# A four-layer graph attention stack: list pieces moved out of the head, lists three row tiles ahead, masks kept as bits

## The chip, the cores and the metric

The kernel runs on one core of a Trainium2 chip. The metric is the device time of one execution in microseconds (us). Five engines work side by side, each through its own queue of instructions: PE (TensorE, matmuls), DVE (VectorE), ACT (ScalarE), POOL (GpSimd, which here issues the indirect gathers) and SP (SyncE, which here issues most of the other DMAs).

## The reference

N = 4096 nodes with F = 256 features, and an adjacency matrix `adj` that is a random 1/256 of all pairs plus the diagonal, so that a row has about 17 neighbours. Four attention layers follow each other, each inside `x = layernorm(x + layer(x))`. Every layer has this form (layer 0 is shown; layer 1 is alike, layer 2 has two heads of 128 and biases, layer 3 has one score, a positive and a negative softmax over `x` itself, a matrix product and an ELU):

```python
h = (x @ W.T).reshape(4096, 4, 64).transpose(1, 0, 2)
e = alpha_src[:, :, None] + alpha_dst[:, None, :]      # two inner products of h per head
e = jnp.where(e >= 0, e, 0.2 * e)
e = jnp.where(adj[None, :, :] == 0, -jnp.inf, e)
attn = jax.nn.softmax(e, axis=-1)
out = jnp.einsum('hij,hjd->hid', attn, h)              # 4 heads of 64, put side by side
```

The same `adj` masks all four layers.

## The kernel before

**Tiles.** The 4096 nodes are 32 row tiles of 128 rows; four row tiles make a block. Instead of all 4096 columns, a row tile works on lists of the columns that its 128 rows need. A class `Projection` makes the projected rows of one row tile (values, scores and, in layer 0, the adjacency bits of that node) and stores them in the memory tables `vals` and `edge`. A class `RowTile` loads the rows on the lists of one row tile: one direct load of its own 128 rows and 13 indirect gathers on POOL (L763) of 128 rows each, into the buffers `G`. It works in two halves: half 0 reads its own rows and 6 gathers from the first 23 row tiles' rows (MIX = 23), half 1 has 7 gathers from all rows. For each half DVE and ACT form the scores (L871, L876, L880), DVE applies the mask (L837), and PE multiplies by the gathered values (L898). `finish` normalises the row tile, and the projection of the next layer follows.

**The lists.** `lists()` is a generator that builds, block by block and row tile by row tile, the list of columns. For a block: `fetch` loads the raw int32 adjacency (DMAs of 512 KB on SP, 4 buffers), `bytes` turns it to bytes on ACT (L393), `squeeze` folds bytes to bits on DVE (L405) and, for blocks with whole rows, stores the bytes in `maskW`; `sort`, `count`, `add` and `starts` make the counts. For a row tile: `ranks`, `steps`, `spread` (PE), `compare` (DVE, L504), `sum` (26 small matmuls, L516 and L518), and `write` (DVE, L522), which writes the 13 columns of `idx` that the gathers of that row tile read. Each `next(lists)` does one piece. The first five pieces load the block of row tiles 0 to 3 and the first part of the next block; four pieces follow for each row tile.

**The head.** `Program.run` first makes the 32 projections of layer 0, six steps each (transpose, copy, multiply, row, edge, store), as a software pipeline of 37 turns. 21 pieces of the generator (5 + 4 LEAD, LEAD = 4) are woven into these turns. Then the loop over the row tiles of layer 0 takes two pieces for each half, so the lists stay LEAD row tiles ahead. In layer 0, `Layer.part` starts the loads of row tiles up to m + 2 when row tile m is worked on; in the other layers up to m + 1.

**Masks.** In layer 0 the adjacency bits come with the gathered rows. `unpack` spreads them to bytes in a PSUM bank (L798, three instructions per half); a copy of the bank goes to `mk` (L822), and `mk` is stored to `maskC` in memory (L824). Layers 1 to 3 load `mk` from `maskC` (L757); layer 1 copies it to the bank (L826), and layers 2 and 3 multiply by it where it lies.

**Whole rows.** A few blocks of layers 1 to 3 (`WHOLE`: block 7; blocks 3, 7 and 6; blocks 7 and 6) are computed over all 32 column tiles without lists, woven between the row tiles (L1170 to L1181, and L1241 to L1246 for layer 1). Their masks are loaded as bytes from `maskW`, 512 KB for every four column tiles (`mw`).

**Order.** Each engine runs its instructions in the order in which the build placed them. That order isn't the order of the source: the tile scheduler takes an instruction ahead of others where its operands and its output buffer let it. Waits between engines and for DMAs are semaphores that the scheduler adds.

Of the kernel before, what the change touches and what calls it, by code (L numbers as in the profile page):

```python
# [50 lines left out]
P = 128  # L51
# [31 lines left out]
LEAD = 4  # L83
MIX = 23
CAP = NPAIR * P
BW = BT * P // 32
# [35 lines left out]
@with_exitstack  # L122
def kernel(ctx: ExitStack, tc: tile.TileContext, ins: dict, out: bass.AP):
    nc = tc.nc
    const = ctx.enter_context(tc.tile_pool(name="const", bufs=1))
    dram = ctx.enter_context(tc.tile_pool(name="xs", bufs=1, space=DRAM))
    ident = const.tile([P, P], F32, name="ident")
    make_identity(nc, ident)
    shared = {
        "ident": ident,  # L130
        "idx": const.tile([P, NT, NP], I32, name="idx"),
        "mhalf": const.tile([P, BT], F32, name="mhalf"),
        "flag": const.tile([1, 1], I32, name="flag"),
        "shift1": const.tile([P, 1], F32, name="shift1"),
        "shift2": const.tile([P, 1], F32, name="shift2"),
        "shift30": const.tile([P, 1], F32, name="shift30"),
        "shift3": const.tile([4, 4], F32, name="shift3"),
        "zero": const.tile([4, 4], F32, name="zero"),
        "maskC": dram.tile([NT, P, NU, P], U8, name="maskC"),
        "maskW": dram.tile([NB, P, NT, BT, P], U8, name="maskW"),  # L140
        "d": [const.tile([P, NT, TERMS[n]], F32, name=f"d{n}") if WHOLE[n] else None for n in range(4)],
        "v": [[dram.tile([N + 1, ROW[n]], F32, name=f"vals{n}{c}") for c in range(1 if n else 2)] for n in range(4)],
        "e": [dram.tile([NT, TERMS[n], P], F32, name=f"edge{n}") for n in range(4)],
        "x": [None] + [dram.tile([N, F], F32, name=f"xp{n}") for n in (1, 2, 3)],
    }
    nc.vector.memset(shared["mhalf"], -0.5)
    nc.vector.memset(shared["shift1"], -KEXP)
    nc.vector.memset(shared["shift2"], -2.0 * KEXP)
    nc.vector.memset(shared["shift30"], -3.0 * KEXP)

    nc.vector.memset(shared["zero"], 0.0)
    nc.vector.memset(shared["shift3"], -2.0 * KEXP)
    nc.gpsimd.affine_select(out=shared["shift3"], in_=shared["shift3"], pattern=[[1, 4]], compare_op=ALU.is_gt,
                            fill=0.0, base=0, channel_multiplier=-1)
    with ExitStack() as packed:
        Program(tc, packed, ins, out, shared).run()
    general = nc.values_load(shared["flag"][0:1, 0:1], min_val=0, max_val=1,
                             skip_runtime_bounds_check_because="it is the result of a comparison")
    with tc.If(general > 0):
        dense_layers(tc, ins, out, ident)  # L160
# [18 lines left out]
class Program:  # L179
# [99 lines left out]
    def lists(self, ctx):  # L279
# [62 lines left out]
        pat = cst.tile([P, 8, P // 32], I32, name="pat")  # L342
# [16 lines left out]
        shared["pat"] = pat  # L359
# [13 lines left out]
        class Block:  # L373
# [21 lines left out]
            def squeeze(self, part):  # L395
                js = slice(part * JG, (part + 1) * JG)
                if any(self.blk in w for w in WHOLE):
                    nc.sync.dma_start(out=shared["maskW"][self.blk, :, js], in_=self.mk)
# [9 lines left out]
                if part == BT - 1:  # L408
                    rows = shared["v"][0][self.blk % 2][:N, :BW].rearrange("(j p) w -> p j w", p=P)
                    nc.sync.dma_start(out=rows, in_=self.bits.rearrange("p j t w -> p j (t w)").bitcast(F32))  # L410

# [188 lines left out]
    def run(self):  # L600
# [3 lines left out]
        for n in range(4):  # L604
            for v in self.shared["v"][n]:
                nc.sync.dma_start(out=v[N:N + 1, :], in_=nothing[:, :ROW[n]])
        w0 = self.weights(0)
        layer = Layer(self, 0)
        with ExitStack() as ctx:
            lists = self.lists(ctx)  # L610
            xs = []
            for q in range(NT // 2):
                if q % 4 == 0:
                    slot = self.g0.tile([P, SLOT], F32, name="G")
                c = 2 * F * (q % 4)
                nc.sync.dma_start(out=slot[:, c:c + 2 * F].rearrange("p (t f) -> p t f", t=2),
                                  in_=to_tiles(ins["x"][2 * q * P:2 * (q + 1) * P, :]))
                xs += [slot[:, c:c + F], slot[:, c + F:c + 2 * F]]

            line = [Projection(self, 0, w0, x, m, (self.ptwo[0], self.ptwo[1], self.pmask)) for m, x in enumerate(xs)]  # L620
            turns, ahead, listed = NT + 5, BT + 1 + 4 * LEAD, 0
            for m in range(turns):
                while listed < ahead and listed * turns <= m * ahead:
                    next(lists)
                    listed += 1
                for k, step in enumerate(Projection.STEPS):
                    if 0 <= m - k < NT:
                        step(line[m - k])

# [8 lines left out]
        self.mwp = self.pool("mwp", 2)  # L638
# [5 lines left out]
        layer.close(None)  # L644


class Projection:
# [61 lines left out]
    def store(self):  # L709
        n, nc, T = self.n, self.nc, TERMS[self.n]  # L710
        erow = self.prog.io.tile([4, P], F32, name="erow")
        shift = self.shared["shift3"] if n < 3 else self.shared["zero"]
        nc.scalar.activation(erow[:T, :], self.pe[:T, :P], AF.Identity, bias=shift[:T, LOGS[n]:LOGS[n] + 1])
        nc.sync.dma_start(out=self.shared["e"][n][self.m], in_=erow[:T, :])
# [8 lines left out]
class RowTile:  # L723
# [23 lines left out]
    def load(self, half):  # L747
# [4 lines left out]
        if half == 0:  # L752
            self.S = prog.ld.tile([P, H4, P], F32, name="S")
            nc.sync.dma_start(out=self.S[:, :TERMS[n]], in_=sh["e"][n][m].partition_broadcast(P))
            self.mk = prog.ld.tile([P, NU, P], U8, name="mk")
            if n > 0:
                nc.sync.dma_start(out=self.mk, in_=sh["maskC"][m])  # L757
# [22 lines left out]
    def unpack(self, half, words):  # L780

        nc, pat = self.layer.nc, self.layer.shared["pat"]
        rows = self.slot(half, 0)[:, :HALF * ROW[0]].bitcast(I32).rearrange("p (k c) -> p k c", k=HALF)
        bits = rows[:, :, self.m % BT * (P // 32):(self.m % BT + 1) * (P // 32)]
        own = 1 - half
        two = 2 * len(PAIRS[half])
        for s in range(2):
            u = PAIRS[half][0]
            self.spread(words[:, u:u + two // 2, s * P // 8:(s + 1) * P // 8],
                        bits[:, own + s:own + two:2], pat[:, 4 * s:4 * (s + 1)])  # L790
        u, k = FULL[half][0], 0 if own else two
        count = len(FULL[half])
        self.spread(words[:, u:u + count, :], bits[:, k:k + count], pat)

    def spread(self, words, bits, pat):
        count, planes = bits.shape[1], pat.shape[1]
        shape = [P, count, planes, P // 32]
        self.layer.nc.vector.tensor_tensor(  # L798
            words.rearrange("p t (k w) -> p t k w", k=planes),
            bits.rearrange("p t (o w) -> p t o w", o=1).to_broadcast(shape),  # L800
            pat.rearrange("p (o k) w -> p o k w", o=1).to_broadcast(shape), op=ALU.bitwise_and)

    def half(self, half):
# [8 lines left out]
        first = half * UNITS[0]  # L812
        mh = self.mk[:, first:first + U, :]
        if n < 2:
# [4 lines left out]
            kept = mh.rearrange("p t i -> p (t i)").bitcast(I32)  # L819
            if n == 0:  # L820
                self.unpack(half, there.rearrange("p (t i) -> p t i", t=U))
                nc.vector.tensor_scalar(kept, there, 0, None, op0=ALU.bitwise_or)  # L822
                if half == 1:
                    nc.sync.dma_start(out=sh["maskC"][self.m], in_=self.mk)  # L824
            else:
                nc.vector.tensor_scalar(there, kept, 0, None, op0=ALU.bitwise_or)  # L826
            mh = there.bitcast(U8)
            mh2 = mh.rearrange("p (o i) -> p o i", o=1).to_broadcast([P, 2, U * P])
        pairs = [prog.wp.tile([P, 2, UNITS[1], P], F32, name="w") for _ in range(H // 2)]
# [93 lines left out]
class Layer:  # L923
# [47 lines left out]
    def part(self, m, part):  # L971


        if part == 0:
# [3 lines left out]
            for q in range(m, m + (3 if self.n == 0 else 2)):  # L978
# [7 lines left out]
    def half_alone(self, m, part):  # L986
# [4 lines left out]
        second = m > NT - (LEAD if self.n == 0 else 6) and len(self.ready) > 1  # L991
# [144 lines left out]
    def whole_rows(self):  # L1136
# [3 lines left out]
        for blk in WHOLE[n]:  # L1140
            tiles = range(blk * BT, (blk + 1) * BT)
            S = prog.bk.tile([P, T, BT, P], F32, name="Sw")
            for it, m in enumerate(tiles):
                nc.sync.dma_start(out=S[:, :, it, :], in_=sh["e"][n][m].partition_broadcast(P))
            zs = [None] * BT
            for heads in groups:
                accs = [prog.bank(prog.pfour) for _ in range(BT)]
                c0, c1 = heads[0] * Wd, (heads[-1] + 1) * Wd
                vs, mws = {}, {}

                def fetch(j):
                    if j >= NT:
                        return
                    if j % JG == 0:
                        mws[j] = prog.mwp.tile([P, JG, BT, P], U8, name="mw")
                        nc.sync.dma_start(out=mws[j], in_=sh["maskW"][blk, :, j:j + JG])
# [5 lines left out]
                for j in range(NT):  # L1162
                    fetch(j + 4)
                    mj = mws[j - j % JG][:, j % JG, :, :]
# [32 lines left out]
    def whole_heads(self):  # L1197
# [7 lines left out]
        for blk in WHOLE[n]:  # L1205
# [9 lines left out]
            for h in range(A, T):  # L1215
                nc.vector.reciprocal(S[:, h], S[:, h])
                nc.vector.tensor_scalar(S[:, h], S[:, h], LEAST, HUGE, op0=ALU.mult, op1=ALU.min)
            z = prog.bk.tile([P, BT, H, Wd], F32, name="zh")
            for up, flat in TWOS:
                bu, bf = prog.bank(prog.pwhole), prog.bank(prog.pwhole)  # L1220
                vs, mws = {}, {}

                def fetch(j):
                    if j >= NT:
                        return
                    if j % JG == 0:
                        mws[j] = prog.mwp.tile([P, JG, BT, P], U8, name="mw")
                        nc.sync.dma_start(out=mws[j], in_=sh["maskW"][blk, :, j:j + JG])
# [5 lines left out]
                for j in range(NT):  # L1234
                    fetch(j + 4)
                    mj = mws[j - j % JG][:, j % JG, :, :]
# [20 lines left out]
            for it, m in enumerate(tiles):  # L1257
                self.finish(m, z[:, it].rearrange("p h c -> p (h c)"), self.load_x(m), None)

# [547 lines left out]
```

## Time and profile before

| | us |
|---|---|
| median of 3 runs (2065.28 to 2066.7) | 2065.5 |
| the profiled execution | 2071.33 |
| its span, from first to last record | 2069.6 |
| mean granted TensorE clock of it | 0.912 |
| half 1 of row tile 0: first gather | 165.34 |
| row tile 1, row tile 31 of layer 0: first gathers | 174.08, 680.78 |
| layer 1: first gather | 698.2 |

How to read it: the page gives the busy time of each engine and its share of the span. "idle before" of an instruction is the time in which its engine did nothing ahead of it, and what follows "<-" is what ended that time: an instruction of another engine, a DMA, or "issue" where the profile shows nothing that was waited for. L numbers are lines of the kernel before. A busy share over the whole span mixes stages: the head (up to 165 us), layer 0 (to about 698), layer 1 (to about 1160), layer 2 (to about 1540) and layer 3.

### The profile page before, as it was taken

The numbers are of one execution on the slowest core, as the hardware profiler recorded it, in microseconds if no ns is written. First come the engines' busy times: TensorE is split into PE (matmuls) and PEld (weight loads), VectorE is DVE, ScalarE is ACT, GpSimd is POOL, SyncE is SP. The second block draws the span as 40 slices with busy tenths as digits, with TensorE's granted clock in tenths as the row PEclk, the third lists the DMA queues.
The fourth block names the chain that finished last, engine by engine and source line by source line (L and its number), as shares of the span: only waits on it lengthen the run. The fifth ranks groups of instructions, "written<-read, shape, count | busy, mean of one in ns | idle before, by whom it ended". The sixth has DMA issues, their size and how long they took to land. (4 is left out here: it accounts for less than half of the span.)

```text
span 2069.6 us, 46290 instructions
## 1 busy us (share of the span) xinstructions
PE 1822.6 (88%) x15281; PEld 1509.8 (73%) x15281; DVE 1467.9 (71%) x4366; ACT 1500.9 (73%) x4659; POOL 1383.9 (67%) x1387
## 2 busy tenths in 40 slices
PE   4765798999899959989989998899998999999995
PEld 2444677777778859978878788788986677667773
DVE  2434888888888959977777867778876366575655
ACT  4436888888877948866767769878874687667873
POOL 0016777777777777777777767777762776666772
PEclk7666998989989979998999999999999899999998
DMA  8677999999986867766666766777875898888983
GB/s 287 177 187 253 316 300 328 269 294 318 328 207 179 236 197 201 207 191 188 192 187 187 203 176 187 231 209 229 233 205 188 262 297 274 261 289 276 294 254 109
DMA packets 297816, 486.59 MB, mean 235 GB/s; under 512 B 77815, under 2 KB 206940, under 8 KB 297565
## 3 DMA queue, kind: packets, MB, share of 16 engines
q1 hardware_dynamic: 218076, 251.50, 40.1%
q0 software_dynamic: 74880, 227.83, 38.0%
q10 hardware_dynamic: 4608, 4.20, 0.6%
q8 instruction: 123, 2.02, 0.4%
q14 instruction: 129, 1.05, 0.2%
HBM read 427.36 MB, written 55.99 MB: 234 GB/s over the span
## 5 line engine op out<-in xcount | busy, mean ns | idle before, releaser
L763 POOL DMA_INDIRECT G<-vals,idx x1352 | 1378.4, 1020 | 653.4 <-issue 348.9
L898 PE MATMUL bank<-G,w 128*64 128x130 f32 (+5 forms) x9156 | 943.5, 311 | 73.6 <-DVE w L837 64.2
L898 PEld LDWEIGHTS bank<-G,w 128*64 128x64 f32 (+1 forms) x9156 | 769.8, 162 | 226.3 <-DVE w L837 73.3
L880 ACT ACTIVATE w<-S,G 128x64 f32<-128x64 f32 (+1 forms) x3080 | 823.5, 351 | 133.2 <-DMA G<-vals,idx 84.2
L1181 PE MATMUL bank<-vw,pw 128*128 128x129 f32 (+1 forms) x2560 | 419.8, 322 | 17.5 <-DVE pw L1171 5.8
L1181 PEld LDWEIGHTS bank<-vw,pw 128*128 128x128 f32 x2560 | 374.1, 194 | 58.2 <-issue 16.0
L837 DVE SCALAR_TENSOR_TENSOR w<-w,bank 128x1024 f32<-128x1024 f32 (+1 forms) x240 | 322.5, 1344 | 13.0 <-ACT w L880 12.4
L673 PE MATMUL bank<-wext,xT 128*128 128x268 f32 (+3 forms) x640 | 188.3, 429 | 33.5 <-DVE row L699 24.1
L673 PEld LDWEIGHTS bank<-wext,xT 128*128 128x128 f32 x640 | 123.2, 210 | 61.2 <-DVE row L699 24.7
L847 ACT ACTIVATE w<-S,G 128x64 f32<-128x64 f32 (+1 forms) x329 | 105.3, 352 | 85.5 <-DMA G<-vals,idx 51.0
L1171 DVE SCALAR_TENSOR_TENSOR pw<-pw,mw 128x512 f32<-128x512 f32 x192 | 129.9, 687 | 36.9 <-ACT pw L1170 35.5
L1178 DVE TENSOR_TENSOR pw<-pw,mw 128x512 f32<-128x512 f32 x128 | 87.6, 688 | 96.1 <-ACT pw L1175 62.8
L393 ACT ACTIVATE mk<-raw 128x1024 uint8<-128x1024 int32 x128 | 130.3, 1051 | 32.6 <-DMA raw<-in_adjB_dram 32.3
L876 DVE TENSOR_TENSOR w<-S,G 128x384 f32<-128x384 f32 x180 | 92.4, 517 | 79.8 <-DMA G<-vals,idx 61.0
L1170 ACT ACTIVATE pw<-Sw,d 128x512 f32<-128x512 f32 x192 | 134.5, 710 | 15.5 <-PE bank L1181 10.2
L1244 PE MATMUL bank<-vw,pw 128*128 128x65 f32 x512 | 89.1, 257 | 19.9 <-issue 19.9
L1173 ACT ACTIVATE pw<-Sw,d 128x512 f32<-128x512 f32 x128 | 89.9, 708 | 19.3 <-DMA Sw<-edge 10.3
L1246 PE MATMUL bank<-pw,vw 128*65 128x128 f32 x512 | 99.5, 277 | 0.0
L1244 PEld LDWEIGHTS bank<-vw,pw 128*128 128x128 f32 x512 | 78.6, 194 | 27.6 <-issue 27.3
L1241 DVE SCALAR_TENSOR_TENSOR pw<-Sw,cw,mw 128x512 f32<-128x512 f32 x128 | 93.8, 740 | 0.0
L664 ACT COPY xT<-bank 128x256 f32<-128x256 f32 x128 | 46.3, 362 | 62.3 <-PE bank L659 41.0
L706 PE MATMUL bank<-ident,row 128*4 128x128 f32 (+2 forms) x128 | 37.6, 294 | 56.6 <-DVE row L693 30.5
(193 smaller groups left out, 1805.1 us busy)
## 6 DMA issues: line engine op xcount, KB each, us to landing
raw<-in_adjB_dram SPq DMA_DIRECT2D x128, 512.0 KB
G<-vals,idx POOLq DMA_INDIRECT x1352
mw<-maskW SPq DMA_DIRECT2D x36, 512.0 KB
vw<-vals SPq DMA_DIRECT2D x128, 128.5 KB
S<-edge SPq DMA_DIRECT2D x60, 256.0 KB
vals<-row SPq DMA_DIRECT2D x96, 134.0 KB
vw<-vals SPq DMA_DIRECT2D x96, 129.0 KB
xp<-y SPq DMA_DIRECT2D x96, 128.0 KB
```

Of the source, the lines that this page charges most:

```text
L393: nc.scalar.activation(self.mk[:, 2 * q:2 * q + 2], src, AF.Copy)
L673: nc.tensor.matmul(pp[:, :c1 - c0], self.xT[:, k, :], wext[:, k, c0:c1], start=(k == 0), stop=(k == KT - 1 and brow is None))
L763: nc.gpsimd.indirect_dma_start(out=self.row(half, k), out_offset=None, in_=self.values[:N + 1 if half else MIX * P, :], in_offset=bass.Ind ...
L837: nc.vector.scalar_tensor_tensor(pair, pair, LEAST, mh2, op0=ALU.max, op1=ALU.mult)
L847: nc.scalar.activation(w[0][:, u, rows], S[:, 0, rows], AF.Relu, bias=d(g, 0))
L880: nc.scalar.activation(w[h][:, u, rows], S[:, h, rows], AF.Exp, bias=d(g, h))
L898: nc.tensor.matmul(a, w[h][:, u, rows], b, start=half == 0 and u == 0 and (n == 3 or h == turns[0][0]), stop=half == 1, skip_group_check=True)
L1170: nc.scalar.activation(p, S[:, h], AF.Exp, bias=d)
L1171: nc.vector.scalar_tensor_tensor(p, p, LEAST, mj, op0=ALU.max, op1=ALU.mult)
L1181: nc.tensor.matmul(accs[it][:, c:c + Wd], p[:, it, :], v[:, c:c + Wd], start=(j == 0 and h == heads[0]), stop=(j == NT - 1), skip_group_ch ...
L1244: nc.tensor.matmul(bu[:, it * Wd:(it + 1) * Wd], p[up][:, it, :], v[:, up * Wd:(up + 1) * Wd], start=j == 0 and it == 0, **how)
L1246: nc.tensor.matmul(bf[:Wd, it * P:(it + 1) * P], v[:, flat * Wd:(flat + 1) * Wd], p[flat][:, it, :], start=j == 0 and it == 0, **how)
```

## The change

- `LEAD` goes from 4 to 3, and layer 0 starts loads up to row tile m + 1 instead of m + 2. A constant `LATE` keeps the 4 that another condition took from `LEAD`.
- Nine list pieces (block of row tiles 0 to 3, the first part of the next, and row tile 0's own list) are woven into the first 24 turns of the head; the other eight of the 17 pieces follow when all projections have been issued.
- The x tiles of the head come in 6 loads instead of 16; the zero rows of `vals` are stored from ACT's queue instead of SP's; layer 0's `edge` rows are stored four row tiles at a time (8 stores instead of 32).
- `maskC` and `maskW` (bytes) become `bitsC` and `bitsW` (32-bit words of bits). A row tile's bits take 28 words a partition instead of bytes for all columns; a block's bits take 256 KB and are loaded once for each whole unit.
- In layer 0, `unpack` first copies the bits out of the gathered rows into a tile `bits` and stores it; the spread to bytes reads `bits`, and nothing is copied back from PSUM. In layers 1 to 3 the spread is done again for every half (three instructions), and once for every column tile of a whole unit (`bytes`).

The number of gathers (1352) is the same. The core of the diff:

```diff
-LEAD = 4
+LEAD = 3
+LATE = 4
...
-        "maskC": dram.tile([NT, P, NU, P], U8, name="maskC"),
-        "maskW": dram.tile([NB, P, NT, BT, P], U8, name="maskW"),
+        "bitsC": dram.tile([NT, P, 2 * HALF, MW], I32, name="bitsC"),
+        "bitsW": dram.tile([NB, P, NT, BT, MW], I32, name="bitsW"),
...
-            turns, ahead, listed = NT + 5, BT + 1 + 4 * LEAD, 0
+            turns, soon, listed = NT + 5, BT + 5, 0
             for m in range(turns):
-                while listed < ahead and listed * turns <= m * ahead:
+                while listed < soon and listed * 24 <= m * soon:
                     next(lists)
                     listed += 1
                 for k, step in enumerate(Projection.STEPS):
                     if 0 <= m - k < NT:
                         step(line[m - k])
+            for _ in range(BT + 1 + 4 * LEAD - listed):
+                next(lists)
...
     def unpack(self, half, words):
-        rows = self.slot(half, 0)[:, :HALF * ROW[0]].bitcast(I32).rearrange("p (k c) -> p k c", k=HALF)
-        bits = rows[:, :, self.m % BT * (P // 32):(self.m % BT + 1) * (P // 32)]
+        bits = self.bits[:, half * HALF:(half + 1) * HALF]
+        if L.n == 0:
+            t = self.m % BT * MW
+            rows = self.slot(half, 0)[:, :HALF * ROW[0]].bitcast(I32).rearrange("p (k c) -> p k c", k=HALF)
+            L.nc.vector.tensor_scalar(bits, rows[:, :, t:t + MW], 0, None, op0=ALU.bitwise_or)
+            if half == 1:
+                L.nc.sync.dma_start(out=L.shared["bitsC"][self.m], in_=self.bits)
...
-            if n == 0:
-                self.unpack(half, there.rearrange("p (t i) -> p t i", t=U))
-                nc.vector.tensor_scalar(kept, there, 0, None, op0=ALU.bitwise_or)
-                if half == 1:
-                    nc.sync.dma_start(out=sh["maskC"][self.m], in_=self.mk)
-            else:
-                nc.vector.tensor_scalar(there, kept, 0, None, op0=ALU.bitwise_or)
+            self.unpack(half, there.rearrange("p (t i) -> p t i", t=U))
...
+        else:
+            there = prog.mkp.tile([P, UNITS[1], P // 4], I32, name="mk")[:, :U]
+            self.unpack(half, there)
...
-            for q in range(m, m + (3 if self.n == 0 else 2)):
+            for q in (m, m + 1):
...
-                    mj = mws[j - j % JG][:, j % JG, :, :]
+                    mj = self.bytes(bits, j)
...
+    def block_bits(self, blk):
+        bits = self.prog.mwp.tile([P, NT, BT, MW], I32, name="bw")
+        self.nc.sync.dma_start(out=bits, in_=self.shared["bitsW"][blk])
+        return bits
+
+    def bytes(self, bits, j):
+        mj = self.prog.mup.tile([P, BT, P // 4], I32, name="mw")
+        spread(self.nc, mj, bits[:, j], self.shared["pat"])
+        return mj.rearrange("p t i -> p (t i)").bitcast(U8).rearrange("p (t i) -> p t i", t=BT)
```

## Prediction

> **What bounds the kernel now.** I read the page first, then the waits by engine, then windows by stage, then the timeline where the stages meet. The page's busy shares name PE:
>
> ```profile
> PE 1822.6 (88%) x15281; PEld 1509.8 (73%) x15281; DVE 1467.9 (71%) x4366; ACT 1500.9 (73%) x4659; POOL 1383.9 (67%) x1387
> L763 POOL DMA_INDIRECT G<-vals,idx x1352 | 1378.4, 1020 | 653.4 <-issue 348.9
> ```
>
> That is a mean over unlike stages. The windows (PE, PEld, DVE, ACT, POOL busy, then PE clock, DMA share, GB/s) separate them:
>
> ```profile
> 100.00:150.00 50.00, 29.59 (x144) 20.00 (x143) 15.78 (x58) 21.83 (x65) 5.96 (x6) 0.70 0.84 216
> 300.00:350.00 50.00, 43.47 (x421) 35.08 (x421) 40.30 (x128) 40.23 (x134) 38.11 (x39) 0.86 1.04 285
> 600.00:650.00 50.00, 48.26 (x477) 39.63 (x477) 40.62 (x133) 38.43 (x152) 37.97 (x39) 0.90 0.68 188
> 1400.00:1500.00 100.00, 97.24 (x868) 91.29 (x867) 82.57 (x243) 83.22 (x241) 78.03 (x73) 0.98 0.80 228
> 1900.00:2000.00 100.00, 98.88 (x538) 73.54 (x536) 64.43 (x198) 80.87 (x183) 72.64 (x70) 1.00 0.90 288
> ```
>
> Layers 2 and 3 (last two lines) are PE's. In layer 0 POOL makes 39 gathers in 50 us, as fast as it can: the timeline (start, duration, idle before) shows a period of 0.95 + 0.30 = 1.25 us,
>
> ```profile
> 641.33 0.95 POOL L763 DMA_INDIRECT G<-vals,idx  x1 [0.31 <-DVE y L1304]
> 642.59 0.95 POOL L763 DMA_INDIRECT G<-vals,idx  x1 [0.30 <-issue]
> ```
>
> so 13 x 1.25 = 16.25 us for a row tile. Its first gathers stand at 174.08 for tile 1 and 680.78 for tile 31: 506.7/30 = 16.89 us per tile. PE, DVE and ACT need about 14.8, 13.7 and 14.7 us of each. From 165 us to about 1160 us (end of layer 1) **POOL's gathers set the time**; any microsecond in which POOL waits there is lost. Before 165 us it waits for the head:
>
> ```profile
> POOL G L763 <- issue: 348.9, 1112, 9.2
> POOL G L763 <- DVE bits L405: 120.1, 2, 119.8
> POOL G L763 <- DMA edge<-erow: 33.0, 2, 32.6
> ```
>
> The 32.6 is the stop at 132.7: half 1 of tile 0 may read any row, so it waits for the last projection row (DVE, 162.31), its store, and starts at 165.34. Nowhere is there a wait for `idx` (L522): the lists are ahead of POOL everywhere.
>
> **What the skill says.** Perfetto Trace Analysis, "DMA Instruction — SWDGE (GPSIMD)": the bar of such a DMA ends with the last descriptor, not with the data. The trace agrees: in the timeline the last gather of a half ends at 185.47 + 0.95 + 3 x 1.25 = 190.17, its reader starts at
>
> ```profile
> 195.79 0.56 DVE L876 TENSOR_TENSOR w<-S,G 128x384 f32<-128x384 f32 x1 [9.23 <-DMA G<-vals,idx]
> ```
>
> which is 5.6 us later. Nine such pairs in layer 1, where raw blocks no longer load, give 2.0 to 4.0, mean 3.1 us. DMA: Bandwidth & Descriptors, "Anatomy of one DMA — SWDGE (gpsimd) path", gives a fixed 2.0 us; the trace's lower end agrees, its loaded end is longer. I take L = 4.5 us, both ends 3 and 6. DVE: scalar operands, raw-bit mode, write accounting and state across instructions, "5. Flops that outlive an instruction", calls DVE's queue one in-order queue; the trace shows nothing against that. All that follows rests on it: what stands behind a waiting DVE instruction waits too.
>
> **The head.** Nine list pieces instead of 21 stand among the projections. In the built order 26 of 32 projection rows now precede the seventh squeeze and the last precedes the eighth; before, the last followed the ninth. Raw loads ahead of the last row store fall from 37 to 30 (19.4 to 15.7 MB); at the 216 to 286 GB/s of the head, 3.7 MB are 13 to 17 us. The rest comes from projection steps that no longer queue behind list rows on DVE, ACT and SP (PE is busy 59% there, DVE 32%). SP also loses 5 zero stores (to ACT's queue), 10 of 16 x loads and 24 of 32 edge stores. Estimate: half 1 of tile 0 starts at about 118 instead of 165.3, **-47 us**; ends 105 and 140 (-60, -25).
>
> **The lists in layer 0.** This is what decides. With LEAD 4, the write of an index stood well ahead of its gathers. With LEAD 3 it is one tile nearer, and the change adds `bits<-G`, a copy that reads all 14 rows of a half and so waits for that half's last gather. Its output is tiny (28 words a partition), its buffers are free early, and the built program places it far ahead of its use. DVE's order after the change, around tile 12 (row numbers of that order):
>
> ```
> 585 bits<-G x3 (halves 11.1, 12.0, 12.1)   617 bits<-G (half 13.1)
> 586 masked w (10.1)                        618 masked w ... 625 spread
> 589-595 spreads, folds, d                  622-641 folds, sort, compares, masked
> 597 idx write of tile 13                   645 idx write of tile 14
> ```
>
> Gather 13 needs row 597; row 597 stands behind row 585; row 585 waits until the last gather of tile 12 has **landed**. POOL has then nothing to issue: it stops for L and for what DVE and PE do between the copy and the index. In the order before, the index of tile 9 is written while tile 6 is worked on, with no instruction ahead of it that waits for tile 8. The pattern stands at tiles 4, 5, 6, 9, 10, 13, 14, 17, 18, 21, 22, 25 and 26: 13 places. From tile 28 the lists are exhausted and the indices run ahead.
>
> Price of one place, from rows of before:
> - Short (tiles 4, 5, 9, 13, 17, 21, 25): masked multiply 1.48 (L837, 1280 wide), 14 matmuls about 2.9 (half of the 5.8 of a half), edge 0.4, 26 small list matmuls (L516, L518) about 3.0, index write and hand-over 0.4: 8.1 + L.
> - Long (10, 14, 18, 22, 26): some 28 DVE rows, with folds (0.68 + 0.41 + 0.28), sort, two compares (0.65 each) and further masked multiplies: about 11.5 + L. Tile 6 about 10 + L.
> - Sum: 7 x 8.1 + 5 x 11.5 + 10 = 124, and 13 L = 58: 182 us; the next two indices of a group of four are 1 to 2 us late at each of five groups, +10. **+192 us**. Ends: L = 3 and 2 us less per place 192 - 20 - 26 = 146; L = 6 and 2 us more, 238.
>
> Checked as a timeline of first gathers, started at 118: tile 4 at about 189 (before 224), 6 at 249 (258), 8 at 284 (292), 10 at 346 (325), 14 at 443 (393), 18 at 540 (461), 26 at 734 (598), 31 at 819 (681). The head's gain is used up by tile 9; the end of layer 0 is 138 us later, near 192 - 47 = 145. I take +140.
>
> **Masks as bits.** Layer 0 loses two copies per tile (L822, 0.28 and 0.31) and gains two `bits<-G` of about 0.15 (the small copies L695): -0.3 us of DVE, hidden. Layer 1 puts three spreads (0.192 + 0.213 + 0.213, L798) in place of one copy (L826, 0.30) in 56 halves, and 64 block spreads of about 0.28 (nearest row: the 128x128 fold): 17 + 18 = 35 us of DVE, at 76 to 78% busy beside POOL. Layer 2: 40 x 0.61 + 96 x 0.28 = 51; layer 3: 48 x 0.61 + 128 x 0.28 = 65. DVE goes from 77% to about 90% of layer 2's 400 us and from 65% to 77% of layer 3's 500; PE stays the bound. Covered by the gathers and PE's matmuls; if the cover is gone, the new spread sits between landing and masked product, at most 51 us in layer 2. I take **+10**, ends 0 and 50. Against it stand some 33 MB fewer of 487 MB moved (mask blocks 18.9 MB, kept masks 8.6, their stores 11, less some 5 new); at a DMA share of 0.8 to 0.9 I take **-5**, ends -15 and 0. New waits: the bit stores on SP wait for copies that run early, and nobody waits behind them; block bits of 256 KB come once per unit instead of every fourth step.
>
> Sum: 140 + 10 - 5 = +145, with 3 us at the seam of layers 0 and 1, where two gathers of layer 1 now stand ahead of tile 31's last 13: **+148**. The profiled execution took 2071.3 us (span 2069.6), so 2219; it stood 5.8 us over the median of the runs, so **2213 us**.
>
> **Rivals.**
> 1. *Shorter stops, 0.20:* L is 2 to 3, and the rows between copy and index have mostly run while DVE waited; a place costs 7 us. 13 x 7 - 47 + 5 = +49 to +80: 2115 to 2145. For it: the 2.0 us landings of layer 1. Against: rows 586 to 597 are behind the copy in the queue.
> 2. *Longer, 0.20:* the stops let PE and DVE starve, then everything queues for DVE; long places 20 us, landings 6 under raw loads (DMA share 1.04 in layer 0), layer 2 DVE-bound: +200, about 2265. For it: PE already waits up to 13.2 us for L837 in the waits of before.
> 3. *Faster, 0.04:* the gathers run more than a tile ahead of DVE's copies, so that a copy never waits. Then only the head remains: -47 + 5, about 2024. It decides where `idx` of tile m+1 is written before tile m's last gather is issued. Against it: rows 585 and 597, and DVE's habit in the trace (195.79 above) of taking up a half the moment it lands.
> 4. *The head isn't shorter, 0.06:* raw loads bound it and half 1 still starts near 150: +180, 2245.
>
> **How the numbers follow.** The likeliest case has 0.50 (2175 to 2250), the rivals 0.20, 0.20, 0.04, 0.06. Range 2110 to 2280, which leaves out the fast case and the tails of rivals 1 and 2. A measurement of this kernel tells about 0.2% (4 us) from no change. Faster by more than that has 0.04, within it 0.01, slower 0.95.
>
> **What would show it.** Right: POOL waits of 10 to 17 us for the `idx` write at some 13 places between 150 and 750 us; DVE `bits<-G` waiting on DMA G; 26 to 30 gathers instead of 39 per 50 us; layer 1 starting near 830 instead of 698; the first half-1 gather near 118; layers 1 to 3 no longer than before by over 20 us. Wrong: POOL still at 39 gathers per 50 us in layer 0, or layers 2 and 3 that have grown with a DVE over 95% busy.

## The result and the profile after

The change makes the kernel slower: 2231.4 us (median of 4 runs, 2228.3 to 2235.0) against 2065.4 (4 runs), a ratio of 1.080 with a 95% interval of 1.0786 to 1.0823. The forecast was 2213 us, in a range of 2110 to 2280. The profiled execution took 2228.3 us, with a span of 2226.6.

The page after (busy time and share of the span; then the group of the gathers and that of the new copies: busy, mean ns, idle time before them and what ended most of it):

```profile
PE 1843.3 (83%) x15281; PEld 1523.8 (68%) x15281; DVE 1546.7 (69%) x5030; ACT 1499.1 (67%) x4659; POOL 1388.5 (62%) x1387
L780 POOL DMA_INDIRECT G<-vals,idx x1352 | 1383.0, 1023 | 806.4 <-issue 397.4
L804 DVE TENSOR_SCALAR bits<-G 128x28 int32<-128x28 int32 x64 | 11.4, 178 | 195.0 <-DMA G<-vals,idx 192.3
```

The gathers (L763, now L780) cost what they did, 1023 ns each; only the idle time before them has grown, from 653 to 806 us. The copies `bits<-G` take 11.4 us of DVE, and DVE stood still for 195 us in front of them. The waits (total, times, longest) say who waited for whom:

```profile
POOL G L780 <- issue: 397.4, 1137, 13.2
POOL G L780 <- DVE idx L524: 95.4, 5, 21.1
POOL G L780 <- ACT mk L395: 34.9, 2, 23.3
DVE bits L804 <- DMA G<-vals,idx: 192.3, 32, 16.5
```

In the kernel before, the only wait put down to `idx` was as short as the usual time between two gathers:

```profile
POOL G L763 <- DVE idx L522: 0.3, 1, 0.3
```

So the long wait for `idx` is new. It is more than the 95.4 us of its line: several stops stand under "issue" (the longest was 9.2 us before, 13.2 now) or under another engine that came last by the trace. In the timeline POOL has exactly 13 stops of over 11 us in layer 0, ahead of tiles 4, 5, 6, 9, 10, 13, 14, 17, 18, 21, 22, 25 and 26, with 214.3 us in all. Two neighbours of them (POOL: last gather before, first after; DVE: the copy and the index write):

```profile
518.31 0.95 POOL L780 DMA_INDIRECT G<-vals,idx  x1 [0.30 <-issue]
531.68 0.94 POOL L780 DMA_INDIRECT G<-vals,idx  x1 [12.43 <-issue]
...
547.01 0.94 POOL L780 DMA_INDIRECT G<-vals,idx  x1 [0.30 <-issue]
566.38 0.94 POOL L780 DMA_INDIRECT G<-vals,idx  x1 [18.42 <-DVE idx L524]
```

```profile
521.68 0.18 DVE L804 TENSOR_SCALAR bits<-G 128x28 int32<-128x28 int32 x1 [8.83 <-DMA G<-vals,idx]
...
530.77 0.17 DVE L524 TENSOR_TENSOR idx<-bank,limit 128x13 int32<-128x13 f32 x1 [3.85 <-PE bank L520]
...
550.42 0.18 DVE L804 TENSOR_SCALAR bits<-G 128x28 int32<-128x28 int32 x1 [7.03 <-DMA G<-vals,idx]
...
565.93 0.17 DVE L524 TENSOR_TENSOR idx<-bank,limit 128x13 int32<-128x13 f32 x1 [2.01 <-ACT counts L439]
```

Read the first stop across both: POOL's last gather ends at 519.25; its data land and let the copy go at 521.68 (2.4 us); DVE and PE then work until the index is written at 530.94 (9.3 us); POOL goes on at 531.68 (0.7 us). The second is 2.5 + 15.7 + 0.3. While POOL stands, everything starves; the windows over two such cycles (PE, PEld, DVE, ACT, POOL, clock, DMA share, GB/s) show all engines low together, where before POOL had 39 gathers in each 50 us:

```profile
500.00:550.00 50.00, 28.48 (x241) 22.99 (x237) 19.42 (x53) 23.19 (x76) 27.30 (x29) 0.70 0.56 172
550.00:600.00 50.00, 44.61 (x448) 36.98 (x448) 42.28 (x131) 41.84 (x141) 25.70 (x27) 0.87 0.92 239
1000.00:1100.00 100.00, 98.53 (x1066) 88.71 (x1065) 91.05 (x258) 76.90 (x300) 77.03 (x76) 1.00 0.67 183
```

The last line is layer 1: DVE is 91% busy, the new spreads among its work, and POOL still makes 76 gathers in 100 us. The same stretch of the kernel before, also in layer 1, had 75:

```profile
1000.00:1100.00 100.00, 90.25 (x955) 81.60 (x954) 78.04 (x186) 66.72 (x256) 77.23 (x75) 0.95 0.69 192
```

The balance of the two profiled spans, by first gathers: tile 1 of layer 0 starts at 137.25 instead of 174.08 (-36.8); from there to gather 417, where layer 1 began before, 723.7 instead of 524.1 (+199.6); the rest 1365.6 instead of 1371.4 (-5.8). Sum: +157.0.

### The profile page after: what moved, and what is told of

It reads as the page before. It is cut to its first block, busy times and chain, and to the rows that moved or that the text cites. A ratio compares the mean times of both kernels' runs of the same rounds, so it can differ in the third digit from the quotient of the medians.

```text
span 2226.6 us, 46785 instructions
## 1 busy us (share of the span) xinstructions
PE 1843.3 (83%) x15281; PEld 1523.8 (68%) x15281; DVE 1546.7 (69%) x5030; ACT 1499.1 (67%) x4659; POOL 1388.5 (62%) x1387
## 4 chain that ended last, share of the span: by engine, by line
PE 35%; POOL 10%; DMA 8%; DVE 6%; issue 5%; ACT 4%; SPq 0%; POOLq 0%; ACTq 0%; DVEq 0%
PE bank L906 17%; PE bank L1187 11%; POOL G L780 10%; DMA G<-vals,idx 6%; PE bank L686 3%; ACT w L888 2%; DVE w L845 1%; PE bank L1250 1%; PE bank L1248 1%; DMA G<-vals 1%; DMA Sw<-edge 1%; ACT pw L1176 1%; PE bank L672 1%; PE bank L689 0%; DVE pw L1177 0%
## 5 line engine op out<-in xcount | busy, mean ns | idle before, releaser
L780 POOL DMA_INDIRECT G<-vals,idx x1352 | 1383.0, 1023 | 806.4 <-issue 397.4
L906 PE MATMUL bank<-G,w 128*64 128x130 f32 (+5 forms) x9156 | 971.9, 316 | 220.2 <-DVE w L845 210.0
L906 PEld LDWEIGHTS bank<-G,w 128*64 128x64 f32 (+1 forms) x9156 | 788.9, 165 | 381.2 <-DVE w L845 226.2
L845 DVE SCALAR_TENSOR_TENSOR w<-w,bank 128x1024 f32<-128x1024 f32 (+1 forms) x240 | 322.8, 1347 | 8.3 <-ACT w L888 7.8
L686 PE MATMUL bank<-wext,xT 128*128 128x268 f32 (+3 forms) x640 | 183.0, 418 | 14.5 <-ACT xT L677 12.0
L804 DVE TENSOR_SCALAR bits<-G 128x28 int32<-128x28 int32 x64 | 11.4, 178 | 195.0 <-DMA G<-vals,idx 192.3
L710 ACT ACTIVATE row<-bank,shift 128x2 f32<-128x2 f32 x64 | 16.6, 259 | 158.3 <-DVE d L708 151.2
L1248 PE MATMUL bank<-vw,pw 128*128 128x65 f32 x512 | 88.9, 257 | 16.3 <-issue 16.3
## 6 DMA issues: line engine op xcount, KB each, us to landing
vw<-vals SPq DMA_DIRECT2D x128, 128.5 KB
vw<-vals SPq DMA_DIRECT2D x96, 129.0 KB
```

Source lines behind the costliest of these rows:

```text
L686: nc.tensor.matmul(pp[:, :c1 - c0], self.xT[:, k, :], wext[:, k, c0:c1], start=(k == 0), stop=(k == KT - 1 and brow is None))
L780: nc.gpsimd.indirect_dma_start(out=self.row(half, k), out_offset=None, in_=self.values[:N + 1 if half else MIX * P, :], in_offset=bass.Ind ...
L845: nc.vector.scalar_tensor_tensor(pair, pair, LEAST, mh2, op0=ALU.max, op1=ALU.mult)
L906: nc.tensor.matmul(a, w[h][:, u, rows], b, start=half == 0 and u == 0 and (n == 3 or h == turns[0][0]), stop=half == 1, skip_group_check=True)
L1248: nc.tensor.matmul(bu[:, it * Wd:(it + 1) * Wd], p[up][:, it, :], v[:, up * Wd:(up + 1) * Wd], start=j == 0 and it == 0, **how)
```

## The experiments

All ratios are to the kernel before on the same chip. "Half 1" is the first gather of half 1 of row tile 0.

**1. The order alone.** One order constraint is added to the changed kernel: on DVE a copy may not be placed before `last_mask`, the masked multiply (L845) that the program text placed last. The core of the edit:

```diff
-            L.nc.vector.tensor_scalar(bits, rows[:, :, t:t + MW], 0, None, op0=ALU.bitwise_or)
+            with ExitStack() as order:
+                if L.prog.last_mask is not None:
+                    order.enter_context(L.prog.tc.issue_after(L.prog.last_mask))
+                L.nc.vector.tensor_scalar(bits, rows[:, :, t:t + MW], 0, None, op0=ALU.bitwise_or)
...
-            nc.vector.scalar_tensor_tensor(pair, pair, LEAST, mh2, op0=ALU.max, op1=ALU.mult)
+            prog.last_mask = nc.vector.scalar_tensor_tensor(pair, pair, LEAST, mh2, op0=ALU.max, op1=ALU.mult).ins
```

> The changed kernel with one ordering constraint more: on DVE's queue a copy bits<-G may not come before the last masked multiply of the half worked on just before it. Work, DMAs, buffers and LEAD = 3 are unchanged. By the built order the write of idx for tile 13 then stands behind the copies up to half 11.0 instead of 12.1, and no index stands behind the copy of the tile just ahead of it. Theory 'copies ahead of the index writes': the 13 stops of POOL (214 us) all but go, layer 1 starts near 665 us, about 2030 us in all (2020 to 2060). Rival 'LEAD = 3 is too short by itself': the indices still come late, 2180 or more. Rival 'the list pieces that follow the projections congest the start of layer 0': the first three stops (54 us) stay and the other ten go, about 2085.

Measured: 2033.3 us, ratio 0.985 (0.982 to 0.988). One stop of 1.6 us is left in layer 0 after 150 us; layer 1 starts at 663.2. The idle time of DVE before the 64 copies falls from 195.0 us to 0.9. The same two windows are full again:

```profile
500.00:550.00 50.00, 45.77 (x471) 38.27 (x473) 44.31 (x124) 48.21 (x158) 38.66 (x38) 0.93 0.87 282
550.00:600.00 50.00, 48.46 (x496) 38.89 (x492) 42.11 (x141) 37.77 (x152) 38.12 (x40) 0.90 0.79 197
```

The same instructions, DMAs, buffers and LEAD take 198 us less. With the copies placed later the scheduler also placed some other rows of DVE elsewhere, so the run alone doesn't separate the copies from these. Experiment 5 reaches nearly the same time by another edit. The first three stops have gone with the other ten, so the late list pieces did not make them either.

**2. LEAD = 4 in the changed kernel** (`LEAD = 3` to `LEAD = 4`, one line).

> The changed kernel with LEAD = 4 again (12 list pieces instead of 8 follow the projections); nothing else is changed. By the built order the copies bits<-G move ahead as well: the index of tile m stands behind the copy of half (m-1).1 at 16 places (6, 8, 9, 10, 12, 13, 14, 16, 17, 18, 20, 21, 22, 24, 25, 26) instead of 13. Theory 'copies ahead of the index writes': not better, about 2230 to 2280 us. Rival 'LEAD = 3 is too short by itself': the stops go, about 2030 us.

Measured: 2276.3 us, ratio 1.102 (1.099 to 1.105). The trace has 16 stops of over 11 us, 246.5 us in all, at the 16 places that the built order names. The stops ahead of tiles 4 and 5 have gone (2.3 us are left at tile 4), and others have come in. Lists that are built earlier don't help on the whole while the scheduler moves the copies ahead with them.

**3. LEAD = 3 in the kernel before** (`LEAD = 3`, and in layer 0 `for q in (m, m + 1)`).

> The kernel before with LEAD = 3 and loads up to row tile m + 1 in layer 0 alone: old head (17 pieces woven in), byte masks, no bits<-G copies. Theory 'copies ahead of the index writes': nothing that waits for tile m-1 stands ahead of the index of tile m, so no stops: 2050 to 2075 us. Rival 'LEAD = 3 is too short by itself': 2200 us or more.

Measured: 2044.7 us, ratio 0.991 (0.988 to 0.994): no stops, and below the expected range. With 17 pieces instead of 21 in the head, half 1 starts at 148.8 instead of 165.3, which is most of the gain. LEAD = 3, with loads up to m + 1, is harmless without the copies.

**4. The head of the change in the kernel before** (weaving, x loads, edge and zero stores as in the diff; LEAD = 4).

> The kernel before with the head of the change alone: nine pieces in 24 turns, the other twelve (LEAD = 4) after the projections, six x loads, edge rows stored four at a time, zero rows from ACT's queue. Byte masks, loads up to m + 2. Theory: the head's 37 us stay to the end, since POOL sets the time through layer 1: 2025 to 2035 us. Rival 'the earlier start is given back, since the lists then come late': 2050 us or more.

Measured: 2040.2 us, ratio 0.989 (0.986 to 0.991). Half 1 starts at 129.5, 36 us earlier; at the start of layer 1 25.5 us of it are left. The time lies above the theory's range and below the rival's: some 10 us go in layer 0, where the twelve late pieces are now worked on. The trace shows 7.8 us of them as four stops of POOL, of 1.0 to 2.3 us, ahead of tiles 14, 18, 22 and 26. There the index is written just before POOL goes on (at tile 14 it is ready at 359.35, and the gather starts at 359.62). So the rival's reason, late lists, holds in a small measure.

**5. One buffer instead of four for layer 0's bits** (a tile `bits0`, `bufs=1`, in place of `bits` where n = 0).

> The changed kernel with one buffer for layer 0's bits tile instead of four, and no other constraint (layers 1 to 3 keep four). The copy of a tile can then not be placed before the spread of the tile ahead of it; by the built order the index of tile 13 stands behind half 11.1, not 12.1: a whole tile of gathers (16.25 us) earlier. Theory 'a stop is landing + DVE and PE rows - gathers still in hand': short stops 12.4 - 16.25 vanish, long ones 18.5 - 16.25 leave about 2 us at six places, tile 4 about 7: 2033 + 15 to 20 = about 2050 us (2040 to 2060). Rival 'any hoisting at all costs the stop': above 2150. Rival 'only the order by hand cures it': 2231.

Measured: 2038.8 us, ratio 0.990 (0.987 to 0.993). That is just below the expected range. Seven stops of over 1 us are left, the longest 4.8, with 16.4 us in all. Fewer buffers cure nearly all that an order by hand cures: the free buffers had let the copies go ahead.

**6. Half a tile between** (the copy held behind the last masked multiply of three halves earlier).

> The changed kernel with the copies bits<-G held behind the last masked multiply of three halves earlier. By the built order the index of tile 13 stands behind half 12.0: seven gathers (8.75 us) less than in the changed kernel. Theory 'a stop is landing + DVE and PE rows - gathers still in hand': seven short stops of 12.4 - 8.75 = 3.7 us, six long ones of 18.5 - 8.75 = 9.7, tile 4 longer by 11: 26 + 58 + 11 = 95 over the first experiment's 2033: about 2128 us (2105 to 2150). Rival 'the stop is there or not': 2231, or 2033.

Measured: 2074.9 us, ratio 1.006 (1.003 to 1.009); 12 stops of 1.1 to 8.7 us between 190 and 610 us, 57.5 us in all. The time is below the expected range: by the ratios it is some 42 us over experiment 1, where 95 were expected. The stop is graded, not there or absent, but at the 13 places of the changed kernel it fell by some 12 us on average, more than the 8.75 us of gathers that were won. The index of tile 14 shows what else changed (DVE, then POOL):

```profile
368.03 0.18 DVE L808 TENSOR_SCALAR bits<-G 128x28 int32<-128x28 int32 x1 [0.49 <-DMA S<-edge]
...
379.96 0.17 DVE L524 TENSOR_TENSOR idx<-bank,limit 128x13 int32<-128x13 f32 x1 [1.92 <-ACT counts L439]
```

```profile
372.76 0.94 POOL L781 DMA_INDIRECT G<-vals,idx  x1 [0.30 <-issue]
380.40 0.94 POOL L781 DMA_INDIRECT G<-vals,idx  x1 [6.70 <-DVE idx L524]
```

From copy to written index it is 12.1 us here, against 17.2 at the same tile of the changed kernel (15.7 at the like tile 18, shown above), and DVE stood idle for only 0.49 us before the copy. That less work has piled up on DVE and PE after a shorter wait is my reading; no run isolates it. My fixed 18.5 us did not allow for it.

**7. The masks as bits alone** (the changed kernel with the old head, LEAD = 4, loads to m + 2, copies held as in experiment 1).

> The masks alone: bits in memory for all layers, spread in every half and whole unit, the copies bits<-G held behind the last masked multiply of the half just before; old head, LEAD = 4, loads up to m + 2. Theory: the added spreads (some 150 us of DVE) hide beside POOL and PE, and 35 MB fewer are moved: layers 1 to 3 some 2 to 6 us shorter, 2058 to 2068 us. Rival 'DVE becomes the bound of layer 2': 2080 or more.

Measured: 2058.2 us, ratio 0.999 (0.998 to 1.001): no difference that the measurement tells. The spreads hide, or the 35 MB that are no longer moved pay for them: the run measures the two together.

**8. The weaving alone, in the kernel before.**

> The kernel before with the weaving alone: nine pieces in 24 turns, the other twelve after the projections; 16 x loads, 32 edge stores and the zero rows on SP as before. The head with all three parts starts half 1 of tile 0 at 129.5 us, the old one at 165.3. Theory 'fewer list pieces and raw loads ahead of the last row': most of the gain stays, half 1 at 130 to 137 us, 2040 to 2048 us. Rival 'SP's small DMAs held the head up': half 1 at 150 us or later, 2055 or more.

Measured: 2043.4 us, ratio 0.992 (0.989 to 0.995). Half 1 starts at 120.9, earlier than with all parts of the head (129.5). The gain of the head is that of the weaving. The changed DMAs cost some 8 us of the earlier start; in the total time the two runs (0.992 and 0.989) can't be told apart.

**9 to 11. Can those 8 us be had?** Experiment 1 with single edge stores, with all old DMAs, and unchanged, on one chip.

> The kernel of the first experiment (copies held late) with the 32 single edge stores of before instead of 8 batched ones; x loads in six and zero rows from ACT's queue stay. By the built order SP then has no raw load among the last 13 row stores, as in the weaving alone (half 1 at 120.9 us); with batched edge stores it has one after every third row store (128.6). Theory 'batching moves raw loads ahead of the last row stores': half 1 at about 121 us, 6 to 10 us less than the first experiment, about 2026 us. Rival 'the x loads made the difference': half 1 stays near 128, 2033 us.

> The kernel of the first experiment with all DMAs of the old head: 16 x loads, 32 edge stores, zero rows from SP. Theory 'batching moves raw loads ahead of the last row stores': like the run with single edge stores, about 2026 us, within 4 us of it. Rival 'the x loads made the difference': 2026 here and 2033 there.

> The kernel of the first experiment unchanged, beside the two others on the same chip: 2033 us, half 1 of tile 0 at 128.6 us.

Measured: 2034.4, 2033.3 and 2034.1 us; ratios 0.986, 0.987 and 0.987, each within 0.0023. The mechanism was right: half 1 starts at 119.7, 122.4 and 129.0, so the edge stores make the difference. In SP's queue 24 raw loads stand ahead of the last row store with single edge stores (experiments 8, 9 and 10) and 30 with batched ones; the other six come one by one among the last row stores. The time was not right: with single edge stores POOL soon meets a late index,

```profile
135.94 0.95 POOL L777 DMA_INDIRECT G<-vals,idx  x1 [0.31 <-issue]
144.60 0.94 POOL L777 DMA_INDIRECT G<-vals,idx  x1 [7.70 <-DVE idx L524]
```

and by tile 4 the three kernels are within 2.7 us (185.5, 188.2, 188.1). In the two with the earlier start, a wait for an index takes most or all of it back (7.7 us above, 7.5 in the run with all old DMAs). The three can't be told apart in time. Experiment 1 and these two are the fastest versions: 1.3 to 1.5% faster than before, 9% faster than the change as made.

## Why the prediction was right

- **The bound and the mechanism: right.** All 13 places, their tiles, the waiting copy and the missing index came as the built order said; experiments 1 and 5 show that the place of the copy decides, and experiments 2 and 3 that LEAD = 3 is not the cause.
- **Price of a stop: two terms mis-sized, against each other.** Landing, from the last gather's bar to the copy: 2.1 to 3.6 us, mean 2.7 at the 13 places, where I took 4.5: -23 us. The 5.6 that I had read was from the wrong gather. ACT takes up the six gathers of that half one by one, the last at 195.64, and by the semaphores that last one is the gather that POOL issues at 190.47, not the one before it; its bar ends at 191.42, so that half waited 4.4 us. Still, 4.5 is near what the kernel before shows in layer 0 (last section); at a stop, where no gather follows, the wait is shorter. From the copy to POOL's next gather: about 10.5 instead of 8.1 for the five later short ones (they stop 13.0 on average), 16.3 instead of 11.5 for long ones (19.1 on average), 20 for tile 4, where rows that prepare layer 1's weights stand in DVE's queue too. For long ones I had added up DVE's rows; the trace shows DVE waiting in them for PE's list matmuls (2.65 us before L506 at 559.22) and for `counts`, which comes from matmuls queued behind those of attention (PE runs them from 565.39, after attention's from 564.36). That is +55 us. The 10 us for further late indices did not show. Sum: 214 instead of 192.
- **Net of layer 0:** +199.6, where 187 (140 and the head's 47) was forecast. Outside the stops a tile takes (723.7 - 214.3)/31 = 16.4 us instead of 16.9.
- **The head: right in kind, 10 us too large** (-36.8, not -47). Half 1 started at 128.5, not 118. I counted the batched edge stores as relief for SP; experiment 9 shows them to cost 9 us of the start. The six raw loads that then come among the last row stores (3.1 MB, 11 to 15 us at the prediction's 216 to 286 GB/s, an estimate) are enough for that.
- **Layers 1 to 3: -5.8 instead of +8** (10 - 5 + 3). The difference can't be told from nothing: experiments 3, 4 and 8, whose layers 1 to 3 are those of the kernel before, took 1361.6 to 1367.0 us for this part. The cover of the spreads held at 91% DVE. Their price was also too high: 35 + 51 + 65 = 151 us summed the bars of single rows, and the bars grew by 157, but neighbouring rows overlap (in the stop ahead of tile 18 a spread that starts at 553.69 lasts 0.20, and the next row starts at 553.81), and DVE was busy only 86 us longer.
- The net of layer 0, the head and the later layers make 12.6 + 10.2 - 13.8 = +9: 157 instead of 148. The other 9 us to the median are the profiled executions: before's stood 6 us over its median, this one 3 under. That the total came out within 1% of the measured time is in part luck: -23, +55, -10, +10 and -14 us partly cancel.
- **Rivals:** the shorter stop was right on landing and wrong on the rows; the longer one was right on the long places (19.1 of 20 us) and wrong on landing and on a layer 2 bound by DVE (83% busy there). The head's rival (no gain) is refuted, and so is "faster", for the kernel as built; experiment 1, where the copies hardly wait, is what that rival described, at 2033 us.

## What to carry to other kernels

On an engine whose queue runs in order, as DVE's does here, a cheap instruction that waits for a DMA can be as dear as what is queued behind it: the copies took 11.4 us and held DVE for 195. Look in the built order for what stands between it and the instruction that feeds the next DMA, since a small output with free buffers invites a scheduler to move it ahead. Here the feeder of the bounding queue (`idx`) stood behind a consumer of the same queue (`bits`), which makes a loop through landing, DVE and PE at each turn. An order constraint or one buffer instead of four breaks it here, and LEAD = 4 does not.

## What the runs showed of the hardware

A gather's data were usable 2.1 to 3.6 us (mean 2.7) after its bar on POOL ended, at the 13 places where no further gather followed. In the kernel before, where gathers follow each other, the semaphore records of the trace (the last increment of a gather's semaphore against the end of its bar) give 1.8 to 9.6 us, 4.9 at the median, over 395 gathers of layer 0, while raw blocks load, and 2.6 at the median over 344 gathers of layer 1. The Trainium skill (DMA: Bandwidth & Descriptors, "Anatomy of one DMA — SWDGE (gpsimd) path") gives a fixed part of about 2.0 us for setup and completion of such a DMA. The waits at the 13 places lie above that, though they are counted only from the end of the bar.

Neighbouring rows on DVE overlap in the trace, so that the sum of their bars is more than DVE's busy time: in layers 1 to 3 the bars grew by 157 us with the change, the busy time by 86.
